# S's products between the pieces of the logits, in a graph attention and nucleus diffusion kernel

## The chip, the cores and the metric

The kernel runs on one core of one Trainium2 chip. The metric is the device time of an execution in microseconds; runs of one kernel are compared by their median.

## The reference

The input is 2708 rows of 512 features and a dense 2708 x 2708 adjacency of zeros and ones. Two layers follow each other. The first is graph attention with eight heads. The second, which the change touches, makes two steps of diffusion. In a step it builds an attention matrix that keeps, in each row, only the largest weights whose sum reaches 0.9 of the row (the nucleus), and it moves three copies of the features: forward and backward with the adjacency, and with the attention matrix.

```python
S = S + jnp.eye(n, dtype=X.dtype)
Rf = S / jnp.clip(S.sum(axis=1, keepdims=True), 1e-12)
Rb = S / jnp.clip(S.sum(axis=0), 1e-12)[:, None]
Xf, Xb, Xa = (X, X, X)
for s in range(STEPS):                     # STEPS = 2
    A = _adj_from_feats(Xa, W1, W2, W3)    # logits, nucleus of 0.9, softmax
    Xf = Rf @ Xf
    Xb = Rb @ Xb
    Xa = A @ Xa
    Z = Z + (Xf @ U1[s] + Xb @ U2[s] + Xa @ U3[s])
Y = X + Z                                  # and a layer norm
```

## The kernel before

Rows are cut into 22 tiles of 128 (the last has 20 rows). A pair is two tiles, a quad four; there are 11 pairs and 6 quads, the last quad of two tiles. Each of the two steps (s = 0 and 1, the flag `last` is the second) runs a loop over g from -1 to 10 in which three pairs are in work at once.

- **Logits of pair g + 2** (`Logits.products`, L513): for each of the two tiles six pieces of 452 columns, each two matmuls into a PSUM tile of `ps_t` (two buffers, tile name `t`) and a copy by ScalarE into the tile `p` (four buffers, so the pair's tiles are those of pair g, whose search must be over).
- **Search for pair g + 1** (`search`, L598): VectorE looks for the threshold of each row. It takes the row's maximum of pair g + 2 on the way (`nmx`, L548), and ends in `finish` with a branch (L890). Its results are the tiles `keep`. In its middle it calls `early` and, before `finish`, `late`, which put other engines' work and some of VectorE's into the program there.
- **Attention of pair g** (`attended`, L1005): twelve groups, six for each tile of the pair. A group transposes up to four blocks of `keep` for the next group (L1016), has ScalarE copy them (tile `at`, L1020), and multiplies those of its own with `va` (L1035). From the fourth group on it also issues steps of `fills`, ScalarE's passes over the logits of pair g + 2 (`exp`, L526): for each tile a root and a full exponential, and then twelve looks (L553), which wait for the thresholds `nth` from GpSimd.
- **Mix of pair g** (`mixed`, L1060): three times four steps over the weights U (L1076), each step followed by one step of `others`, and three fills in each of the first two times.
- **S products** (`part`, L943): the steps of the list `others`. One S product loads 128 rows of the features (`hl`, 512 KB, three buffers) and of S (`s_r`, 256 KB) and makes eight matmuls into four PSUM tiles (L967). In the first step one S product serves both directions, a quad has 22 of them over two iterations, and after the second half, at odd g, eight steps `scaled` follow: ScalarE scales a PSUM tile into `xe` (L977), GpSimd's queue writes it out, VectorE splits it into a high and a low part (L181, L182), and GpSimd's queue writes these. In the second step an iteration has 22 S products and four `scaled`, without the splits.
- **Order of the queues**: inside the step the programs of TensorE, ScalarE, VectorE and the DMA queue of SyncE are in the order in which the code issues them (`manual_schedule`). `paced(steps, n)` issues the next n steps of a list. `diffused` loads the four rows tiles `x` that the mix needs.

In the kernel before, all pieces of a block come one after another, then the queries of pair g + 3 are loaded, and the steps of `others` are issued in the attention groups and in the mix. In the first step a group of the pair's first tile issues one and a group of its second tile two; in the second step only the second tile's groups issue some, two each:

```python
if not last:
    paced(others, 1 + i)
elif i or len(grp) == 1:
    paced(others, (total + 10) // 13)
```

Of the kernel before, what the change touches and what calls it, by code (L numbers as in the profile page):

```python
# [53 lines left out]
def kernel(  # L54
# [37 lines left out]
    pairs = [list(range(g, min(g + G, NT))) for g in range(0, NT, G)]  # L92
# [399 lines left out]
    class Logits:  # L492
# [17 lines left out]
                                      in_=kq_d[self.s][DA:, :, t * P:(t + 1) * P])  # L510
                self.q.append(q)

        def products(self):  # L513
            wide, small, ps_l = self.pools
            for q, t in zip(self.q, self.grp):
                pr = rows[t]
                p = wide.tile([P, N], F32, name="p", bufs=4)
                for c0, c1 in chunks:
                    pl = ps_l.tile([P, 512], F32, name="t")
                    for i in range(2):  # L520
                        nc.tensor.matmul(pl[:, :c1 - c0], lhsT=q[:, i], rhs=self.keys[:, c0:c1],  # L521
                                         start=(i == 0), stop=(i == 1))
                    nc.scalar.copy(p[:pr, c0:c1], pl[:pr, :c1 - c0])  # L523
                self.p.append(p)

        def exp(self, looks=True):  # L526
# [387 lines left out]
    for s in range(STEPS):  # L914
        last = s == STEPS - 1
        with ExitStack() as st:
# [18 lines left out]
            def values():  # L935
                for t in range(NT):
                    nc.sync.dma_start(out=va[:rows[t], t, :], in_=(xa_d if last else va_d)[cols[t], :])
# [53 lines left out]
            def paced(steps, n):  # L991
                for step in steps[:n]:
                    step()
                del steps[:n]

            def diffused(grp):
                out_ = []
                for i in range(2):
                    for t in grp:
                        x = work.tile([P, D], F32, name=f"x{i}")  # L1000
                        nc.sync.dma_start(out=x[:rows[t]], in_=xfb_d[i, cols[t], :])
                        out_.append(x)
                return out_[:len(grp)], out_[len(grp):]

            def attended(grp, keep, rden, fills, others, then):  # L1005

                def turned(i, t, cs):
                    pr = rows[t]
                    pt = ps_t.tile([P, TG, P], F32, name="t")
                    at = work.tile([P, TG, P], F32, name="at")
                    for j, c in enumerate(cs):
                        nc.tensor.transpose(pt[:rows[c], j, :pr], keep[i][:pr, cols[c]], ident[:pr, :pr])  # L1016
                    full = sum(rows[c] == P for c in cs)
                    for r, j0, j1 in ((P, 0, full), (rows[cs[-1]], full, len(cs))):
                        if j0 < j1:
                            nc.scalar.copy(at[:r, j0:j1, :pr], pt[:r, j0:j1, :pr])  # L1020
                    return at

                steps = [(i, t, cs) for i, t in enumerate(grp) for cs in tgroups]
                at = turned(*steps[0])
                xa = []
                total = len(others)
                for n, (i, t, cs) in enumerate(steps):
                    pr = rows[t]
                    nxt = turned(*steps[n + 1]) if n + 1 < len(steps) else then()
                    if n >= 3:  # L1030
                        paced(fills, 1 + i if last else 1 if n > 8 else 2)
                    if cs[0] == 0:
                        pa = ps_a.tile([P, D], F32, name="a")
                    for j, c in enumerate(cs):
                        nc.tensor.matmul(pa[:pr], lhsT=at[:rows[c], j, :pr], rhs=va[:rows[c], c, :],  # L1035
                                         start=(c == 0), stop=(c == NT - 1))
                    if not last:
                        paced(others, 1 + i)
                    elif i or len(grp) == 1:
                        paced(others, (total + 10) // 13)  # L1040
                    if cs[-1] == NT - 1:
                        xa.append(work.tile([P, D], F32, name="xa"))
                        nc.scalar.activation(xa[i][:pr], pa[:pr], AF.Copy, scale=rden[:pr, i:i + 1])  # L1043
                        if not last:
                            nc.gpsimd.dma_start(out=xa_d[cols[t], :], in_=xa[i][:pr])
                    at = nxt
                    yield
                return xa, at
# [8 lines left out]
            def turned_rows(grp, v):  # L1057
                return [transposed(up, ps_t, v[i], rows[t], "v_t") for i, t in enumerate(grp)]
# [105 lines left out]
            with tc.manual_schedule(engines={PE, ACT, DVE, SP}):  # L1164
                counted, spread = ranks() if last else (None, None)
                lg = [Logits(pools, s, grp, keys, rank) for grp in pairs[:1]]
                lg[0].queries()
                lg[0].products()
                steps = lg[0].exp(looks=False)
                if last:  # L1170
                    counted()
                for step in steps:
                    step()
                half = []
                lg += [Logits(pools, s, grp, keys, rank) for grp in pairs[1:2]]
                lg[1].queries()
                for step in part(half, 0):
                    step()
                values()
                done = []  # L1180
                ready = None
                looks, left = [], []
                for g in range(-1, NP):

                    fills = []

                    held = len(left)
                    paced(left, held if last else held // 2)
                    others = left + part(half, g + 2)
                    left = []  # L1190
                    if g == 0 and last:
                        paced(others, 4)
                    if g + 2 < NP:
                        lg[g + 2].products()
                    if g + 3 < NP:
                        lg.append(Logits(pools, s, pairs[g + 3], keys, rank))
                        lg[g + 3].queries()
                    norms = [normed(t, y) for t, y in done] if last else []
                    done = []

                    rows_in = []
                    if g >= 0:
                        others.insert(0 if g else len(others) // 3, lambda g=g: rows_in.extend(diffused(pairs[g])))
                        final = g == NP - 1 and not last
                        att = attended(pairs[g], *ready, fills, others,
                                       lambda: None if final else turned_rows(pairs[g], rows_in[0]))
                    if g == 0:

                        paced(others, held - held // 2 if not last else 0)
                        while looks:  # L1210
                            next(att)
                            paced(looks, 2)

                    def early(g=g):
                        if g + 2 < NP:
                            fills.extend(lg[g + 2].exp())
                        return lambda: [rest() for rest in norms]

                    def late(g=g):
                        if g >= 0:  # L1220
                            if g:
                                paced(others, 1)
                            xa, v_t = rest_of(att)
                            done.extend(mixed(pairs[g], v_t, *rows_in, xa, others, fills, final))
                            paced(others, len(others))
                            paced(fills, len(fills))
                            return


                        if last:  # L1230
                            spread()
                        paced(fills, 5 + G * NA)
                        paced(others, NT if last else NT - NT // 2)
                        looks.extend(fills)
                        left.extend(others)

                    if g + 1 < NP:
                        ready = search(lg[g + 1], g >= 0, early, late)
                    else:
                        for rest in norms:  # L1240
                            rest()
                        late()
                if last:
                    for rest in [normed(t, y) for t, y in done]:
                        rest()
# [31 lines left out]
```

## Time and profile before

| what | value |
|---|---|
| median of 3 runs | 3711.15 us (3710.86 to 3714.24) |
| the profiled execution | 3711.47 us, span 3709.7 us |
| busy share of the span | PE 91%, DVE 70%, ACT 42%, POOL 22% |
| mean granted clock of TensorE | 0.963 |
| first step, g = 1 to 8: start of a block of logits to the next | 101.9 to 109.4 us |
| second step, g = 1 to 8, the same | 115.5 to 117.5 us |

The span runs from the first to the last instruction. PE is TensorE, ACT is ScalarE, DVE is VectorE, POOL is GpSimd and SP is SyncE; an engine's name with a q is its sequencer. In a row of groups the first number after the bar is the busy time, the second the mean of one instruction in ns, and after the second bar stands the idle time of the engine just before these instructions, with what ended it. In a timeline the columns are start, duration, engine, line, operation, operands, and in brackets the idle time before and what ended it. The ends of matmuls are modelled, so distances between starts are used here where a pace is meant. The windows give for each stretch the busy time of PE, its weight loads, DVE, ACT and POOL, the granted clock, the share of the DMA engines and GB/s.

The first step of the second layer runs from 1095 to 2304 us of the span, the second from 2304 us to its end.

### The profile page before, as it was taken

Reading aid. Unit: us, or ns where it says so; the run is one execution under the profiler, and the core shown is the slowest. Engines: PE = TensorE matmul, PEld = TensorE weight load, DVE = VectorE, ACT = ScalarE, POOL = GpSimd, SP = SyncE. Lnnn points to the kernel's source line nnn. Section 1 sums busy time; section 2 is a strip of 40 time slices with the busy share of each in tenths; the row PEclk is TensorE's granted clock in tenths of the full one; section 3 lists DMA queues with packets and bytes.
Section 4 is the critical chain, followed back from the end, with each engine's and each line's share of the span. In section 5 each row is a group of like instructions: output and inputs, shape, how many; then the busy total and the mean of one; then the engine's idle time right before and its main releaser. Section 6 shows DMA issues by size and latency. Waiting matters only on the chain. (4 is left out here: it accounts for less than half of the span.)

```text
span 3709.7 us, 35331 instructions
## 1 busy us (share of the span) xinstructions
PE 3376.1 (91%) x11143; PEld 1757.7 (47%) x11143; DVE 2612.0 (70%) x4820; ACT 1541.7 (42%) x2334; POOL 808.4 (22%) x1119
## 2 busy tenths in 40 slices
PE   7998999998956898989899899678999999999898
PEld 4432333333434455545455453445555565556452
DVE  4587888989947537374454652958978779777991
ACT  2343212111124764555666612335654556445511
POOL 4114240514331121121211121301112112121101
PEclk9999999999978999999999999999999999999999
DMA  3476424233237454454545353855655666566652
GB/s 113 152 251 239 141 79 151 82 104 106 70 99 274 139 195 166 156 179 148 199 149 189 122 193 104 302 191 195 206 188 205 234 216 204 184 212 234 202 200 66
DMA packets 276458, 634.08 MB, mean 171 GB/s; under 512 B 37209, under 2 KB 70441, under 8 KB 273243
## 3 DMA queue, kind: packets, MB, share of 16 engines
q1 hardware_dynamic: 249183, 540.99, 44.4%
q0 software_dynamic: 27024, 90.30, 6.4%
q8 instruction: 89, 1.46, 0.2%
q14 instruction: 162, 1.33, 0.1%
HBM read 509.07 MB, written 122.10 MB: 170 GB/s over the span
## 5 line engine op out<-in xcount | busy, mean ns | idle before, releaser
L1035 PE MATMUL a<-va,at 128*128 128x512 f32 (+2 forms) x1936 | 895.6, 602 | 39.6 <-ACT at L1020 39.5
L967 PE MATMUL q<-hl,s_r 128*128 128x512 f32 x2904 | 824.5, 430 | 61.1 <-DMA s_r<-s_d 60.9
L429 PE MATMUL po<-e,fw 128*65 128x512 f32 (+4 forms) x2112 | 838.9, 552 | 32.9 <-DVE e L427 23.3
L427 DVE SCALAR_TENSOR_TENSOR e<-r_b,kk,a_c 128x512 f32<-128x512 f32 (+4 forms) x1056 | 751.1, 740 | 68.5 <-PE po L429 18.1
L967 PEld LDWEIGHTS q<-hl,s_r 128*128 128x128 f32 x2904 | 547.9, 191 | 306.3 <-issue 135.4
L553 ACT ACTIVATE junk_a<-p,nth 128x2708 uint8<-128x2708 f32 (+1 forms) x240 | 613.2, 2555 | 68.8 <-POOL nth L572 65.1
L429 PEld LDWEIGHTS po<-e,fw 128*65 128x65 f32 (+1 forms) x2112 | 285.9, 139 | 546.6 <-issue 270.8
L1035 PEld LDWEIGHTS a<-va,at 128*128 128x128 f32 (+2 forms) x1936 | 339.2, 188 | 408.5 <-issue 346.7
L1076 PE MATMUL a<-u_k,v_t 128*128 128x512 f32 (+1 forms) x1056 | 491.4, 603 | 19.6 <-ACT xa L1043 14.4
L629 DVE SCALAR_TENSOR_TENSOR junk<-p,th 128x2708 bf16<-128x2708 f32 (+1 forms) x132 | 401.3, 3040 | 4.0
L1020 ACT COPY at<-t 128x512 f32<-128x512 f32 (+3 forms) x308 | 140.4, 477 | 478.6 <-PE t L1016 478.4
L1076 PEld LDWEIGHTS a<-u_k,v_t 128*128 128x128 f32 (+1 forms) x1056 | 189.4, 187 | 240.6 <-issue 183.8
L521 PE MATMUL t<-keys,q_t 128*128 128x452 f32 x528 | 165.3, 439 | 94.7 <-ACT p L523 73.6
L181 DVE TENSOR_SCALAR split_hl<-xe 128x512 int32<-128x512 int32 (+1 forms) x44 | 19.1, 434 | 263.4 <-ACT xe L977 217.0
L808 DVE MAX8 vn<-keep 128x8 f32<-128x2708 f32 (+1 forms) x66 | 196.8, 2981 | 2.3
L523 ACT COPY p<-t 128x452 f32<-128x452 f32 (+2 forms) x264 | 132.2, 539 | 123.2 <-PE t L521 85.6
L411 ACT ACTIVATE s_c<-a_c 128x512 fp32r<-128x512 f32 (+3 forms) x132 | 76.2, 578 | 250.1 <-DMA a_c<-in_adj_t_dram 124.8
L1016 PE MATMUL t<-ident,keep 128*128 128x128 f32 (+1 forms) x968 | 147.4, 274 | 26.4 <-DVE keep L757 18.8
L521 PEld LDWEIGHTS t<-keys,q_t 128*128 128x128 f32 x528 | 90.1, 208 | 165.4 <-ACT p L523 126.4
L1016 PEld LDWEIGHTS t<-ident,keep 128*128 128x128 f32 (+1 forms) x968 | 115.0, 139 | 106.8 <-issue 78.6
L548 DVE TENSOR_REDUCE nmx<-p 128x1 f32<-128x2708 f32 (+1 forms) x44 | 129.1, 2966 | 43.4 <-ACT p L523 43.4
L565 POOL TENSOR_TENSOR x<-sums,powers 128x4 f32<-128x4 f32 x22 | 43.7, 1987 | 507.9 <-ACT p L560 481.9
(296 smaller groups left out, 3160.6 us busy)
## 6 DMA issues: line engine op xcount, KB each, us to landing
s_r<-s_d SPq DMA_DIRECT2D x330, 256.0 KB
hl<-vhl_d SPq DMA_DIRECT2D x132, 512.0 KB
u_k<-in_L_gnn_U_dram SPq DMA_DIRECT2D x264, 256.0 KB
hl<-fhl_d SPq DMA_DIRECT2D x132, 512.0 KB
hl<-bhl_d SPq DMA_DIRECT2D x132, 512.0 KB
arow<-in_adj_dram SPq DMA_DIRECT2D x21, 1354.0 KB
s_d<-s_c SPq DMA_DIRECT2D x88, 256.0 KB
a_c<-in_adj_t_dram SPq DMA_DIRECT2D x84, 256.0 KB
```

The source lines that it names most:

```text
L427: nc.vector.scalar_tensor_tensor(e[:pr, :cw], r_b[:pr, i, :cw], kk[:pr, t, hd:hd + 1], a_c[t][:pr, :cw], op0=OP.max, op1=OP.mult)
L429: nc.tensor.matmul(po[i][:, :cw], lhsT=fw[:pr, t, hd, :], rhs=e[:pr, :cw], start=(t == 0), stop=(t == NT - 1))
L521: nc.tensor.matmul(pl[:, :c1 - c0], lhsT=q[:, i], rhs=self.keys[:, c0:c1], start=(i == 0), stop=(i == 1))
L523: nc.scalar.copy(p[:pr, c0:c1], pl[:pr, :c1 - c0])
L553: nc.scalar.activation(junk[:pr], self.p[i][:pr], func, **kw)
L629: v.scalar_tensor_tensor(junk_b[:pr], ps_[i][:pr], th, ps_[i][:pr], op0=OP.is_ge, op1=OP.mult, accum_out=dst)
L808: v.max(vs, keep[0][:pr])
L967: nc.tensor.matmul(half[j], lhsT=s_r[:, j * P:(j + 1) * P], rhs=hl[:, h], start=(c == 0 and h == 0), stop=(c == NT - 1 and h == 1))
L1016: nc.tensor.transpose(pt[:rows[c], j, :pr], keep[i][:pr, cols[c]], ident[:pr, :pr])
L1020: nc.scalar.copy(at[:r, j0:j1, :pr], pt[:r, j0:j1, :pr])
L1035: nc.tensor.matmul(pa[:pr], lhsT=at[:rows[c], j, :pr], rhs=va[:rows[c], c, :], start=(c == 0), stop=(c == NT - 1))
L1076: nc.tensor.matmul(pz[i][:rows[t]], lhsT=v_t[i][:, k, :rows[t]], rhs=u_k, start=(n == 0 and k == 0), stop=(n == 2 and k == KD - 1))
```

## The change

From g = 1 on, the loads of `diffused` and one S product are issued ahead of the block of logits, and after every second piece one more S product is issued, six in a block. For the first tile of a pair an attention group of the first step now issues no step of `others`, for the second tile one instead of two. `diffused` is put at the head of `others` before the block instead of after it, and `late` issues it only where it has not been issued before (g = 9 and 10).

```diff
@@ class Logits @@
-        def products(self):
+        def products(self, between=lambda: None):
+
             wide, small, ps_l = self.pools
+            pieces = 0
             for q, t in zip(self.q, self.grp):
...
                     nc.scalar.copy(p[:pr, c0:c1], pl[:pr, :c1 - c0])
+                    pieces += 1
+                    if pieces % 2 == 0:
+                        between()
                 self.p.append(p)
@@ attended @@
                     if not last:
-                        paced(others, 1 + i)
+                        paced(others, i)
                     elif i or len(grp) == 1:
                         paced(others, (total + 10) // 13)
@@ the loop over g @@
                     if g == 0 and last:
                         paced(others, 4)
+
+                    rows_in = []
+                    if g >= 0:
+                        others.insert(0 if g else len(others) // 3, lambda g=g: rows_in.extend(diffused(pairs[g])))
                     if g + 2 < NP:
-                        lg[g + 2].products()
+                        if g > 0:
+                            paced(others, 2)
+                        lg[g + 2].products((lambda: paced(others, 1)) if g > 0 else lambda: None)
                     if g + 3 < NP:
                         lg.append(Logits(pools, s, pairs[g + 3], keys, rank))
                         lg[g + 3].queries()
                     norms = [normed(t, y) for t, y in done] if last else []
                     done = []
-
-                    rows_in = []
                     if g >= 0:
-                        others.insert(0 if g else len(others) // 3, lambda g=g: rows_in.extend(diffused(pairs[g])))
                         final = g == NP - 1 and not last
@@ late @@
                         if g >= 0:
-                            if g:
+                            if g and not rows_in:
                                 paced(others, 1)
```

## The prediction

> **What bounds the kernel now.** The page first: PE is busy 91% of the span, so I read what PE does between the blocks of logits, and who holds it up. In section 5 of the page the pieces of the logits and their evictions (busy, mean ns | idle before, releaser):
>
> ```profile
> L521 PE MATMUL t<-keys,q_t 128*128 128x452 f32 x528 | 165.3, 439 | 94.7 <-ACT p L523 73.6 <-DMA q_t<-kq_d 19.1
> L523 ACT COPY p<-t 128x452 f32<-128x452 f32 (+2 forms) x264 | 132.2, 539 | 123.2 <-PE t L521 85.6 <-DVEq L890 36.4 <-DVE ends L653 0.3
> ```
>
> PE waits for the evictions, and these, 36.4 us of the time, for the search on DVE (L890 is its last branch). The timeline of PE shows both kinds of block. In the second step (g = 4, an ordinary block):
>
> ```profile
> 2942.90 1.39 PE L521 MATMUL t<-keys,q_t 128*128 128x452 f32 x4
> 2945.73 1.12 PE L521 MATMUL t<-keys,q_t 128*128 128x452 f32 x4 [1.45 <-ACT p L523]
> 2947.05 1.11 PE L521 MATMUL t<-keys,q_t 128*128 128x452 f32 x4 [0.19 <-ACT p L523]
> ...
> 2952.27 1.10 PE L1016 MATMUL t<-ident,keep 128*128 128x128 f32 x8 [0.18 <-ACT p L523]
> ```
>
> 9.4 us for 24 matmuls that PE can start every 0.207 us (in the trace at 2943.51, 2943.72, 2943.92): with two PSUM tiles, ACT's copies of 0.54 us set the pace. In the first step, g = 4:
>
> ```profile
> 1622.12 1.46 PE L521 MATMUL t<-keys,q_t 128*128 128x452 f32 x4
> 1631.68 7.51 PE L521 MATMUL t<-keys,q_t 128*128 128x452 f32 x20 [8.11 <-ACT p L523]
> 1639.09 1.38 PE L1016 MATMUL t<-ident,keep 128*128 128x128 f32 x8
> ```
>
> and the timelines of DVE and ACT say why:
>
> ```profile
> 1602.98 0.69 DVE L182 TENSOR_TENSOR split_hl<-xe,split_hl 128x512 f32<-128x512 f32 x1
> 1603.59 3.03 DVE L806 SCALAR_TENSOR_TENSOR keep<-p,th 128x2708 f32<-128x2708 f32 x1
> ...
> 1629.59 0.14 DVE L887 TENSOR_SCALAR code_i<-code 1x1 int32<-1x1 f32 x1
> ```
> ```profile
> 1631.09 0.97 ACT L523 COPY p<-t 128x452 f32<-128x452 f32 x2 [7.28 <-DVEq L890]
> ```
>
> In an odd g of the first step DVE splits eight scaled rows, and only then ends the search; PE's third piece starts 28.0 us after the last split's end (1603.67 to 1631.68). So **every second block of the first step hangs on the chain S products, xe copies, splits, search**, not on PE.
>
> **What the Trainium skill says.** "Perfetto Trace Analysis", section "Tensor Engine Instruction (MATMUL, LD_WEIGHTS)": ACT, DVE and GPSIMD queues are strict FIFO. The trace agrees: DVE stands 42.81 us in front of the first split at 1583.46 with the search behind it. "DMA: Bandwidth & Descriptors", section "Anatomy of one DMA": a DMA's semaphore wait is on the issuing sequencer. The trace agrees: SP's timeline has no issue from 2935.3 to 2944.62, where the xb load waits for its tile, then twelve in 7 us. "Perfetto Trace Analysis", section "Roofline": about 435 GB/s for 16 DMA engines; the windows 1524 to 1528 read 409.
>
> **Prices.** One S product is 8 matmuls 0.23 us apart, 1.84 us (an attention step with two takes 7.56 us, 2861.69 to 2869.25, one without 3.88, 2840.45 to 2844.33; half of 3.68). Back to back S products come every 2.56 us (11 in 28.16 us from 1149.38), their loads being the limit at three buffers. Two pieces cost PE 4 x 0.207 = 0.83 us. A root, full or look pass on ACT is 2.68 us with its accumulator read. I call T0 the first transpose (L1016) of an iteration, X its start.
>
> **What changes, counted.** For g = 1 to 8: one S product before the pieces, six between them. First step: of 11 S products 7 then come before T0 and 4 in the second row tile's groups; the first tile's groups get none, and in odd g the scaled rows move to the last two groups (2) and the mix (6). At g = 0 and 9 no S product is ahead of T0; six move from the attention groups to the mix. Second step: (19 + 10)//13 is still 2, so the groups keep 12 and only the mix gives up 7. On SP the x loads and S loads pass the query loads and, in the second step, the xb loads; those are wanted only an iteration, or some 20 us, later: nothing. POOL gets the same DMAs, later: counted with the splits.
>
> **1. Second step, g = 1 to 8.** Now: 9.38 + 7 x 1.84 = 22.3 us. After: 1.84 + 6 x (0.83 + 1.84) = 17.9 if nothing waits. But the first S load stands behind the last u_k, two y_d and four x loads and is issued, at SP's pace of now, some 3.5 us before X. In the block at 1518.84 the x loads and three S products, 3.4 MB, go from 1514.65 to 1529, the first S product by its place among the bytes landing near 1524, 6 us after its issue at 1517.94 (an estimate). So PE waits 2.5 to 3 us: 20.9, gain 1.4 x 8 = **-11 us**. Bounds: no wait, 4.4 x 8 = -35; each of the seven loads late by another 0.3, +6. On DVE, nmx starts 7.1 us after the last copy now (2952.66 to 2959.76), which the longer block just uses up, and DVE idles 9.8 us at the iteration's end: no loss there.
>
> **2. First step, ACT in the attention groups.** Without S products a group is 3.9 us of PE, but ACT has two passes and a copy, 6.1 us. At g = 8, where products have run out, it shows:
>
> ```profile
> 2105.74 3.70 PE L1035 MATMUL a<-va,at 128*128 128x512 f32 x8 [0.44 <-ACT at L1020]
> 2109.27 0.38 PE L1016 MATMUL t<-ident,keep 128*128 128x128 f32 x2
> 2111.43 3.70 PE L1035 MATMUL a<-va,at 128*128 128x512 f32 x8 [1.77 <-ACT at L1020]
> ```
>
> Stepped from T0: PE reaches group 3 at 12.6 and group 6 at 23.0. ACT has group 4's copy at 13.9, then four passes with a copy among them, to 25.6, then group 6's copy, 26.1: PE waits 3.1. The looks need nth from POOL, 6.4 us after the last pass (1880.97 to 1887.55 now, less the read): six of them from 32.0 to 49, and PE waits 0.4 to 0.7 for the copies in groups 8, 9 and 10. Attention ends at 57 (64 now, with seven more S products), the mix and project at 80.5 (even g) or 83.1 (odd g; 94.5 now). This is inside steps 3 to 5.
>
> **3. Odd g to even g.** Looks, scaled copies (xe, 0.68) and v_t copies (0.57) are one queue on ACT. From group 9's copy at 49.7: look 52.4, copy, look 55.5, xe 56.2, two v_t, look 60.1, xe 60.7, xa, two v_t 62.6; then xe and look three times, 72.6, xe 73.3, two v_t 74.5, xe, xe 75.9. The last split ends at 79.6 (a split waits 3.9 us for the write of the second before it), against 76.1 now. PE's third piece is then at T0 + 107.6; PE itself is there at 83.1 + 5.3, after two S products and two pieces. Then come ten pieces with five S products, 5 x 2.67 = 13.3, and the clock. After such a wait PE stays at half speed for a while, as now:
>
> ```profile
> 1842.00:1850.00 8.00, 6.99 (x20) 4.15 (x20) 3.52 (x28) 5.39 (x11) 0.00 (x0) 0.70 0.09 36
> ```
>
> (0.70 is the granted clock: 4.8 of the 8 us at half, 2.4 lost; now hidden by ACT's copies.) T0 to next T0: 107.6 + 15.7 = 123.3, against 112.6, 111.5 and 113.2 (mean 112.4): +10.9. Even to odd: 80.5 + 17.9 + 2.5 of load wait = 100.9, against 98.2: +2.7. Three pairs: **+41**. At g = 8 the S products are half as long: 118.8 against 111.7, then some 80 against 83.2: **+4**. Bounds: the last split 5 us earlier or later, 20 us either way.
>
> **4. g = 0 to 1.** PE now stands 10.3 us before 1248.36 for ACT, with five S products ahead of that wait; they come behind it instead: 9.2, less the 1.9 that ACT waits for PE at 1212.93, and 1 for groups like those of 2: +8.3. The first block of g = 1 grows from 8.73 to 20.4: +11.7. **+20**.
>
> **5. g = 9 to 10.** Now the splits end at 2198.15, 54.8 after T0, and PE, at 2223.47, finds the search just done. After, the last S product is in the mix at T0 + 66, the fourth split ends at 76, the search 25.3 later at 101.3; PE is there at 80.1 and has no S product left. 20.5 more, and 2.4 of clock: **+23** (15 to 27).
>
> **Sum:** -11 + 41 + 4 + 20 + 23 = +77 on the profiled execution's 3711.47 (span 3709.7 and 1.8 around it), which is 0.3 above the median: 3788.
>
> **Rivals.** *The loads come in time* (for: 409 GB/s at the peak; against: x and y_d go first): 24 us in step 1 and 10 in the odd blocks go, 3754; chance 0.22 with its neighbours down to 3720. *The search is not the gate*, and it ends faster: steps 3 and 5 hang on the last scaled copy at T0 + 75.9. Each us that ACT brings it earlier saves some 5 us (three pairs, g = 7 to 8, g = 9 to 10). From 15 us earlier, six looks of 2.68 us fewer ahead of it, the sign turns; at 22 us earlier it is 3788 - 110 = 3678. For: the blocks' own idle, 94.7 us, is then gain. Against: ACT's one queue has the looks first. 0.12. *Worse:* the second step's DVE chain, whose slack is the 9.8 us above, is pushed by late p copies, 5 us in each of 8 iterations: 3828; 0.10. *It does nothing:* waits only change their name, 3711; 0.05. The forecast itself, 3770 to 3810: 0.51.
>
> **Numbers.** About 0.2%, 7 us, can be told from no change. The range, 3712 to 3825, leaves out the faster case, some half of the same and half of the worse one (0.2), and takes in the bounds of steps 1, 3 and 5 but for the corners where all fall on one side. Faster 0.12, same 0.05, slower 0.83.
>
> **What would show it.** Right: x20 of L521 after odd g of the first step becomes runs of 4 with L967 between, after a wait of some 20 us for p L523 with L890 behind it (L523 <- DVEq L890 from 36.4 to above 90); PE waits some 20 us for the search once, at g = 10; L1035 <- at L1020 rises from 39.5 by some 40; the blocks of the second step take 20 to 21 us from first S product to T0 and their iterations 114 to 116 instead of 116.7. Wrong: the splits of an odd g ending before T0 + 65, or even blocks that wait no longer than 8 to 11 us.

## The result, and the profile after

The changed kernel takes 3826.8 us (median of 4 runs, 3825.56 to 3837.11) against 3712.69 us for the kernel before on the same chip: a ratio of 1.0315, 95% interval 1.0301 to 1.033, so 114 us slower. The forecast of 3788 us had the sign right and the first step of the layer nearly so; it was 39 us short, and the time lies just above the range's end of 3825. The error is almost all in the second step, where step 1 of the prediction failed. The profiled execution has a span of 3825.2 us against 3709.7, and these two are compared below.

Lines after the change are those of before plus 2 (the pieces), 5 (search, attention, mix, S products) or more. The groups by line of the changed kernel (after the bars: busy, mean ns, then the idle time before and who ended it):

```profile
L1040 PE MATMUL a<-va,at 128*128 128x512 f32 (+2 forms) x1936 | 909.1, 609 | 66.6 <-ACT at L1025 66.6
L972 PE MATMUL q<-hl,s_r 128*128 128x512 f32 x2904 | 815.4, 427 | 118.1 <-DMA s_r<-s_d 117.6
...
L523 PE MATMUL t<-keys,q_t 128*128 128x452 f32 x528 | 148.2, 407 | 92.0 <-ACT p L525 71.7 <-DMA q_t<-kq_d 20.3
...
L525 ACT COPY p<-t 128x452 f32<-128x452 f32 (+2 forms) x264 | 130.1, 538 | 347.8 <-PE t L523 258.3 <-DVEq L895 82.0 <-DVE cur L671 7.2
```

Two of these groups in the kernel before (the pieces and their copies stand in the prediction):

```profile
L1035 PE MATMUL a<-va,at 128*128 128x512 f32 (+2 forms) x1936 | 895.6, 602 | 39.6 <-ACT at L1020 39.5
L967 PE MATMUL q<-hl,s_r 128*128 128x512 f32 x2904 | 824.5, 430 | 61.1 <-DMA s_r<-s_d 60.9
```

Three readings. PE's wait for the pieces' copies is as long as before (92.0 for 94.7), although S products now lie between the pieces: the copies now wait 82.0 us for the search on DVE (L895), where it was 36.4 (L890 then). PE's wait for the loads of the S products has doubled (118.1; it was 61.1). And the attention groups wait 27 us longer for their own copies (66.6; it was 39.6).

The iterations, from T0 (the first transpose of an iteration) to the next T0, say where the time went (us):

| iterations | before | forecast | after |
|---|---|---|---|
| first step, g = 1, 3, 5 | 112.6, 111.5, 113.2 | 123.3 | 124.0, 124.2, 122.3 |
| first step, g = 2, 4, 6 | 98.5, 98.1, 98.1 | 100.9 | 100.2, 101.2, 101.6 |
| first step, g = 7, 8 | 111.7, 83.2 | 118.8, 80 | 120.3, 80.5 |
| first step, g = 0 | 117.5 | +20 | 139.4 |
| first step, g = 9 | 80.1 | +23 | 104.3 |
| second step, mean of g = 1 to 6 | 117.0 | 115.6 | 119.2 |

The first step lost 93 us where 88 was forecast. The second step lost 21 us, all differences of its iterations added, where a gain of 11 was forecast. This is the whole error but for some 7 us. The six iterations of the last row give 13 of the 21: that of g = 0 has the first longer block and no shorter mix (146.6 for 128.6), that of g = 8 a shorter mix and no block (101.0 for 112.4).

**The search, in the first step.** The timeline of PE in the changed kernel, from the end of the mix of g = 3 to the next T0:

```profile
1652.57 2.57 PE L972 MATMUL q<-hl,s_r 128*128 128x512 f32 x8 [2.44 <-DMA s_r<-s_d]
1654.93 1.71 PE L523 MATMUL t<-keys,q_t 128*128 128x452 f32 x4
1656.44 2.45 PE L972 MATMUL q<-hl,s_r 128*128 128x512 f32 x8
1671.91 1.88 PE L523 MATMUL t<-keys,q_t 128*128 128x452 f32 x4 [13.02 <-ACT p L525]
1673.59 3.62 PE L972 MATMUL q<-hl,s_r 128*128 128x512 f32 x8
1677.00 1.38 PE L523 MATMUL t<-keys,q_t 128*128 128x452 f32 x4
...
1688.05 1.04 PE L1021 MATMUL t<-ident,keep 128*128 128x128 f32 x8
```

The third piece waits 13.02 us, and the other ten pieces, with the five S products between them, come behind the wait. That the wait is for the search, and the search for the splits, the timelines of ACT and DVE show:

```profile
1634.20 0.78 ACT L982 ACTIVATE xe<-q,rinv 128x512 f32<-128x512 f32 x1
1634.78 0.78 ACT L982 ACTIVATE xe<-q,cinv 128x512 f32<-128x512 f32 x1
...
1671.32 0.97 ACT L525 COPY p<-t 128x452 f32<-128x452 f32 x2 [19.75 <-DVEq L895]
```
```profile
1641.70 0.43 DVE L181 TENSOR_SCALAR split_hl<-xe 128x512 int32<-128x512 int32 x1 [3.23 <-DMA bhl_d<-split_hl]
1642.17 0.69 DVE L182 TENSOR_TENSOR split_hl<-xe,split_hl 128x512 f32<-128x512 f32 x1
1642.78 3.03 DVE L811 SCALAR_TENSOR_TENSOR keep<-p,th 128x2708 f32<-128x2708 f32 x1
```

With T0 at 1563.9 the last scaled copy ends at +71.7, the last split at +79.0, and the third piece starts at +108.0, 29.1 us after that split.

**The S loads, in the second step.** PE and SP at the start of an ordinary block (for the T0 of g = 4):

```profile
3034.67 12.61 PE L1081 MATMUL a<-u_k,v_t 128*128 128x512 f32 x29
3052.57 3.75 PE L972 MATMUL q<-hl,s_r 128*128 128x512 f32 x8 [5.29 <-DMA s_r<-s_d]
3056.12 1.31 PE L523 MATMUL t<-keys,q_t 128*128 128x452 f32 x4
3057.27 2.02 PE L972 MATMUL q<-hl,s_r 128*128 128x512 f32 x8
3059.12 0.98 PE L523 MATMUL t<-keys,q_t 128*128 128x452 f32 x4
3059.94 2.01 PE L972 MATMUL q<-hl,s_r 128*128 128x512 f32 x8
```
```profile
3032.70 8.07 SPq L1079 DMA_DIRECT2D u_k<-in_L_gnn_U_dram  x5
3040.82 1.76 SPq L1097 DMA_DIRECT2D xw<-y_d  x2
3042.62 1.86 SPq L1006 DMA_DIRECT2D x<-xfb_d  x4
3044.54 0.46 SPq L966 DMA_DIRECT2D hl<-fhl_d  x1
```

The first S product waits 5.29 us for its load, starts 8.0 us after that load was issued, and then runs at half speed: from its start to the first piece 3.55 us, where the next one takes 1.85. In the six blocks of g = 2 to 7 this wait is 3.3 to 5.3 us, 4.1 in the mean; the block shown has the longest of these (that of g = 1 waits 7.0). From there on a unit is 2.67 us (3057.27 to 3059.94), as forecast. In the windows of the same place the columns after the five engines are the granted clock, the share of the DMA engines and GB/s:

```profile
3042.00:3044.00 2.00, 2.00 (x6) 0.91 (x5) 0.00 (x0) 0.00 (x0) 0.00 (x0) 1.00 0.91 268
3044.00:3046.00 2.00, 2.00 (x6) 0.93 (x5) 0.00 (x0) 0.00 (x0) 0.00 (x0) 1.00 0.89 274
3046.00:3048.00 2.00, 1.27 (x3) 0.21 (x2) 0.00 (x0) 1.17 (x2) 0.88 (x1) 1.00 0.91 298
...
3050.00:3052.00 2.00, 0.00 (x0) 0.00 (x0) 1.72 (x15) 0.00 (x0) 1.35 (x3) 0.50 1.03 408
```

The DMA engines are busy from the y_d and x loads on, but move under 300 GB/s until 3048; and at 3050 the clock is already at 0.50.

### The profile page after: what moved, and what is told of

Same layout as the page of the kernel before. It is cut to its first block, busy times and chain, and to the rows that moved or that the text cites. A ratio compares the mean times of both kernels' runs of the same rounds, so it can differ in the third digit from the quotient of the medians.

```text
span 3825.2 us, 35329 instructions
## 1 busy us (share of the span) xinstructions
PE 3386.5 (89%) x11143; PEld 1789.6 (47%) x11143; DVE 2616.7 (68%) x4820; ACT 1538.9 (40%) x2334; POOL 784.0 (20%) x1119
## 5 line engine op out<-in xcount | busy, mean ns | idle before, releaser
L1040 PE MATMUL a<-va,at 128*128 128x512 f32 (+2 forms) x1936 | 909.1, 609 | 66.6 <-ACT at L1025 66.6
L972 PE MATMUL q<-hl,s_r 128*128 128x512 f32 x2904 | 815.4, 427 | 118.1 <-DMA s_r<-s_d 117.6
L972 PEld LDWEIGHTS q<-hl,s_r 128*128 128x128 f32 x2904 | 559.2, 195 | 334.5 <-issue 112.2
L1040 PEld LDWEIGHTS a<-va,at 128*128 128x128 f32 (+2 forms) x1936 | 343.7, 190 | 446.2 <-issue 359.7
L1081 PE MATMUL a<-u_k,v_t 128*128 128x512 f32 (+1 forms) x1056 | 485.7, 600 | 25.5 <-DMA u_k<-in_L_gnn_U_dram 17.2
L1025 ACT COPY at<-t 128x512 f32<-128x512 f32 (+3 forms) x308 | 139.9, 475 | 437.7 <-PE t L1021 437.7
L523 PE MATMUL t<-keys,q_t 128*128 128x452 f32 x528 | 148.2, 407 | 92.0 <-ACT p L525 71.7
L1021 PE MATMUL t<-ident,keep 128*128 128x128 f32 (+1 forms) x968 | 147.2, 275 | 41.1 <-DVEq L895 29.1
L523 PEld LDWEIGHTS t<-keys,q_t 128*128 128x128 f32 x528 | 105.0, 209 | 125.0 <-ACT p L525 87.1
```

The lines of the kernel that those rows point to most:

```text
L972: nc.tensor.matmul(half[j], lhsT=s_r[:, j * P:(j + 1) * P], rhs=hl[:, h], start=(c == 0 and h == 0), stop=(c == NT - 1 and h == 1))
L1081: nc.tensor.matmul(pz[i][:rows[t]], lhsT=v_t[i][:, k, :rows[t]], rhs=u_k, start=(n == 0 and k == 0), stop=(n == 2 and k == KD - 1))
```

## The experiments

Seven kernels were timed beside the kernel before: the first four below have ratios to a median of 3711.59 us, the last three to 3712.86 us.

**Attention groups alone.** The kernel before with fewer S products in the groups, nothing else:

```diff
-                        paced(others, 1 + i)
+                        paced(others, i)
```

> The kernel before with the second part of the change alone: in the first step the attention groups of a pair's first tile issue no step of others and those of the second tile one; nothing is put between the pieces. Theory (ScalarE's one queue and the splits behind it set the first step): at odd g the eleventh S product is now in the mix at T0 + 79, the eight scaled copies and splits follow at some 2.4 us each, so the last split ends near T0 + 99 and the next T0 comes at 134 instead of 112; even g waits for ScalarE's looks and loses 3 to 4; g = 9 to 10 loses 23, g = 0 to 1 loses 8. Sum some +130: 3840 us, second step unchanged. Rival (the S products ahead of the attention are what costs, by delaying it): without them the time stays within 3705 to 3740.

Measured: 3877.83 us, ratio 1.0448 (1.0426 to 1.047), some 166 us slower, nearly all of it in the first step (iterations of odd g 139.9 to 142.9 us, second step unchanged). The row of the copies, and the timelines of PE and of ACT of this kernel, at the iteration before the T0 of 1712.90:

```profile
L523 ACT COPY p<-t 128x452 f32<-128x452 f32 (+2 forms) x264 | 132.0, 539 | 227.3 <-DVEq L890 141.9 <-PE t L521 82.7 <-DVE ends L653 0.7
```
```profile
1669.45 1.45 PE L521 MATMUL t<-keys,q_t 128*128 128x452 f32 x4
1705.45 7.51 PE L521 MATMUL t<-keys,q_t 128*128 128x452 f32 x20 [34.54 <-ACT p L523]
1712.90 1.34 PE L1016 MATMUL t<-ident,keep 128*128 128x128 f32 x8
```
```profile
1661.33 0.69 ACT L977 ACTIVATE xe<-q,rinv 128x512 f32<-128x512 f32 x1 [4.56 <-DMA xfb_d<-xe]
1668.84 0.27 ACT L165 COPY kq_hl<-t 128x128 f32<-128x128 f32 x1 [6.83 <-PE t L160]
...
1671.01 0.72 ACT L977 ACTIVATE xe<-q,cinv 128x512 f32<-128x512 f32 x1
```

The theory's direction holds and its size was 38 us too low. The last split ends 106.2 to 109.1 us after T0: the last of the eleven S products of an odd g is now at +78 to +81, and the last of the eight scaled copies ends some 19 us after it. The looks are over by then; the copies wait for their own buffers to be written out (4.56 us for the seventh), and the eighth stands on ACT's queue behind the copies of the projection, which wait 6.83 us for PE's mix to end. The splits trail by 8 to 10 us. Then 25.9 us of search, and a block with nothing else to do for PE. Thinning the groups alone is worse than the whole change: the block's S products repay a part of it.

**Blocks alone.** The changed kernel with the old pace in the groups:

```diff
-                        paced(others, i)
+                        paced(others, 1 + i)
```

> The changed kernel with the old pacing of the attention groups, 1 + i: seven S products in each block of logits, and the rest as early in the groups as they were before. Theory: at odd g the four S products left are in groups 0 to 3, the scaled steps in groups 4 to 8, the last split ends near T0 + 60, the search near T0 + 88, before TensorE is at the pieces (T0 + 92): no wait for the search in even blocks, T0 to T0 near 112 at odd g, and g = 9 to 10 costs nothing again. Even g still waits for ScalarE's looks, 104 instead of 98. First step +30 instead of +95, second step as in the changed kernel (+21): some 3763 us, 3745 to 3775. Rival (the interleave itself costs the time, by late loads and the slow clock after waits): above 3800.

Measured: 3765.57 us, ratio 1.0148 (1.013 to 1.0167), within the 3745 to 3775 us of the theory. The timeline of PE in the same block as above, and the row of the copies:

```profile
1644.28 3.66 PE L972 MATMUL q<-hl,s_r 128*128 128x512 f32 x8 [2.37 <-DMA s_r<-s_d]
1647.78 0.99 PE L523 MATMUL t<-keys,q_t 128*128 128x452 f32 x4
1648.61 1.99 PE L972 MATMUL q<-hl,s_r 128*128 128x512 f32 x8
1650.43 0.98 PE L523 MATMUL t<-keys,q_t 128*128 128x452 f32 x4
```
```profile
L525 ACT COPY p<-t 128x452 f32<-128x452 f32 (+2 forms) x264 | 129.8, 538 | 281.9 <-PE t L523 269.8 <-DVE fr L669 6.8 <-DVEq L895 5.1
```

No wait for the search is left in the block: the copies stand 5.1 us for L895. The last S product of an odd g before its block is at T0 + 23.6 and the last split at + 58.1 to 58.3; at g = 9 the iteration is 79.9 us, what it was. So the wait of 13 us and the 24 us of g = 9 come from the thinner groups, not from the blocks. But this kernel is 54 us slower than the one before, too: some 17 us in the second step (the sum of its iterations), 14 us at g = 0, and 9 to 10 us in the even g from 2 to 6 of the first step, whose groups now wait for ACT (L1040 stands 97.1 us for L1025).

**The x loads behind.** The changed kernel; in the second step the four x loads are issued behind the block's seven S products:

```diff
-  others.insert(0 if g else len(others) // 3, ...
+  others.insert((7 if last else 0) if g else len(others) // 3, ...
-                            paced(others, 2)
+                            paced(others, 1 if last else 2)
```

> The changed kernel, with the four x loads of an iteration of the second step issued behind the block's seven S products instead of ahead of them; first step as in the change. Theory (the first S load is late because u_k, y_d and x, 1.8 MB, go ahead of it, and the wait brings half a clock): the first load is issued 1.9 us earlier with 1 MB less ahead of it, the wait of 5.3 us at the block's first S product falls under 2 and the slow clock goes: 4 to 6 us in each of 8 iterations, 3780 to 3795. Rival (the S loads themselves cannot keep the block's pace): the wait moves to the third or fourth S product of the block, gain under 10 us, 3817 or more.

Measured: 3798.54 us, ratio 1.0232 (1.0214 to 1.025), 28 us below the changed kernel and a little above the 3780 to 3795 us of the theory. The second-step blocks, from the last mix matmul to T0, fall from 24.9 to 20.6 us (means of six), and the iterations by the same 4.3 us, from 119.2 to 114.9. The profiled execution (span 3815.1 us) was some 18 us longer than the median, and its first step longer than the changed kernel's by as much; only its second step is read here.

**Three loads early, in one burst.** The changed kernel; the first three S loads of the next iteration are issued in the last third of the second step's mix, each directly ahead of the load of a u_k (`part` split into loads and products):

```diff
+                        if n == 2 and k < 3:
+                            paced(ahead, 1)
                         u_k = up.tile([P, D], F32, name="u_k", bufs=4 if last else 3)
                         nc.sync.dma_start(out=u_k, in_=u[s, k * P:(k + 1) * P, :])
...
```

> The changed kernel, with the loads of the first three S products of the next iteration issued in the mix of the second step, ahead of the last time's first three u_k loads; products where they were. Theory (as for the x loads): they land before the block, which takes 18 us from first S product to T0 instead of 25: 6 us in each of 8 iterations, near 3775. Rival: u_k comes late instead and TensorE waits in the mix (L1081 for u_k, 17 us now, rises by 20 or more), total within 15 us of 3827.

Measured: 3818.66 us, ratio 1.0281 (1.0262 to 1.0301): the rival. The blocks fell to 18.2 to 18.6 us as the theory said, the mix rose from 26.6 to between 30.0 and 33.4, and PE's wait for u_k from 17.2 us to 43.8. The end of a mix in the timeline of PE (L1097 is the mix in this kernel, L986 the S products):

```profile
3047.64 1.98 PE L1097 MATMUL a<-u_k,v_t 128*128 128x512 f32 x4 [0.66 <-DMA u_k<-in_L_gnn_U_dram]
3053.37 5.20 PE L1097 MATMUL a<-u_k,v_t 128*128 128x512 f32 x8 [3.74 <-DMA u_k<-in_L_gnn_U_dram]
3058.00 2.40 PE L986 MATMUL q<-hl,s_r 128*128 128x512 f32 x8
```

The weights u_k now stand behind the S loads: the wait has moved one stage up, and the clock has gone to half there (0.50 from 3053.00 to 3056.41; 5.20 us for eight matmuls).

**The second step alone.** The first step as before, with the old pace in its groups and its x loads where they were; S products between the pieces only where `last`:

```diff
...
+                        if last and g > 0:
+                            paced(others, 2)
+                        lg[g + 2].products((lambda: paced(others, 1)) if last and g > 0 else lambda: None)
```

> The first step is as before; only the second step's S products of a block stand between the pieces, as in the change. Theory (the first S load of a block comes late behind the last u_k, two y_d and four x loads, whatever the first step does): the blocks of the second step still take 24 to 26 us, the second step costs some 21 us as in the changed kernel and the first step nothing, so 3730 to 3737 us. Rival (the second step's loss was a consequence of the first step's new order, and step 1 of the prediction holds by itself): blocks of 21 us and 3701 us.

Measured: 3732.27 us, ratio 1.0055 (1.0041 to 1.0068). As the theory said: 19 us slower by itself, iterations 118.2 us (mean of g = 1 to 6), blocks of 22.2 to 25.5 us, first step as in the kernel before. The failure of step 1 of the prediction doesn't come from the first step of the layer.

**The second step alone, x loads behind.** The edits of the two kernels together.

> As the one before, with the four x loads of a second-step iteration issued behind the block's seven S products instead of ahead of them, and one step instead of two ahead of the pieces. Theory: the gain of 28 us that this had on the changed kernel is had here too, blocks of 20 to 22 us, 3702 to 3710 us: within 0.3% of the kernel before. Rival (what was gained there came from the first step, or the x rows now come too late for the transposes of v_t): no better than second_only.

Measured: 3699.72 us, ratio 0.9964 (0.9953 to 0.9974): 13 us faster than the kernel before, a little under what was expected. SP and PE at the block for the T0 of g = 4:

```profile
2936.71 1.52 SPq L1097 DMA_DIRECT2D xw<-y_d  x2
2938.27 0.47 SPq L966 DMA_DIRECT2D hl<-fhl_d  x1
```
```profile
2945.21 2.09 PE L972 MATMUL q<-hl,s_r 128*128 128x512 f32 x8 [1.95 <-DMA s_r<-s_d]
2947.14 0.98 PE L523 MATMUL t<-keys,q_t 128*128 128x452 f32 x4
2947.96 2.02 PE L972 MATMUL q<-hl,s_r 128*128 128x512 f32 x8
```

The load still goes behind y_d and u_k, but PE waits for it 1.95 us here and 1.2 in the mean of the six blocks, against 3.7 in the kernel before this one. The S product after it runs at full speed: the granted clock is 1.00 from 2606 to 3476 us. From the first S product to T0 five of the six blocks take 17.8 to 17.9 us. The x rows come in time: from T0 to the mix it stays at 67.7 us.

**The second step alone, three loads spread over the mix.** As the kernel of three early loads, with the first step of before, and one load every three weight steps, each behind the load of a u_k:

```diff
+                        if (n, k) in ((1, 0), (1, 3), (2, 2)):
+                            paced(ahead, 1)
```

> As second_only, with the first three S loads of a block issued during the mix of the iteration before, one every three weight steps, instead of after it. Theory (the block needs its first three loads early, and the mix has DMA room for 2.4 MB in 26 us if they don't come in one burst): blocks of 18 us with a mix that stays at 26.5 to 28 us, T0 to T0 112 to 113 us instead of 118 to 119, 3675 to 3695 us, faster than the kernel before. Rival (any load in the mix holds up the weights u_k behind it on the same queue, as in the burst): mix of 30 us or more, 3705 to 3725 us.

Measured: 3698.19 us, ratio 0.9962 (0.9948 to 0.9975). Faster than the kernel before the change and than the changed one, and not to be told from the second step alone with the x loads behind. It is 3 us above what was expected. PE at the seam (L1097 is the mix, L986 the S products):

```profile
2921.47 12.18 PE L1097 MATMUL a<-u_k,v_t 128*128 128x512 f32 x28
2935.71 1.99 PE L1097 MATMUL a<-u_k,v_t 128*128 128x512 f32 x4 [2.05 <-DMA u_k<-in_L_gnn_U_dram]
2937.13 2.42 PE L986 MATMUL q<-hl,s_r 128*128 128x512 f32 x8
2939.39 0.98 PE L523 MATMUL t<-keys,q_t 128*128 128x452 f32 x4
```

The block starts without a wait and takes 18.2 us in five of six iterations, but one u_k still comes 2.05 us late, the mix is 27.7 to 28.9 us, and T0 to T0 is 114.6 us, not 112 to 113.

## Why the prediction was right in the first step and wrong in the second

**Step 1 failed, in the term of the load wait and by a term that it left out.** Its sum was 3 us of wait for the first S load and 17.9 us from there to T0, 20.9 in all. Measured, as means of g = 2 to 7: 4.7 us from the start of the mix's last matmul to the first S product, and 20.2 us from there to T0, 24.9 in all. So each block misses 1.7 us of wait and 2.3 us behind it; the eight blocks together are 30 us longer than forecast.

*The wait.* The prediction had the load issued 3.5 us before PE comes, and there 6 us after the issue. In the block shown it was issued 2.7 us before PE had ended its mix (3044.54 to 3047.28), and the S product started 8.0 us after the issue. The 6 us came from a block of the first step, where only the four x loads go directly ahead; here two y_d loads and the last u_k do as well, and the windows read 268 to 298 GB/s. The Trainium skill, "DMA: Bandwidth & Descriptors", section "Queues, rings and completion order", says that on each DMA engine descriptors are consumed in ring order. The trace agrees: the packets of hl, the only ones of 4 KB that move on SP's queue here, begin at 3048.25, 3.7 us after the issue, and until then packets of 2 KB go, the size of the rows ahead. That the x loads are part of it is shown: in the second step alone, with them behind, the mean wait falls from 3.7 to 1.2 us.

*The clock.* Steps 3 and 5 counted 2.4 us of half speed after a wait of PE; step 1 counted none. It is the larger part: with the clock at 1.00, the second step alone with the x loads behind takes the 17.9 us that the step had said. The Trainium skill, "TensorE: Matmul & The Clock Gate", section "Part 1: The HAM clock gate", says that the clock drops to half after an idle window of some 3.4 us, and that this window runs freely. The trace agrees on the second point: in the changed kernel half speed begins at 2691.62, 2814.50, 2930.55 and 3050.02, whole multiples of 3.413 us apart (36, 34 and 35). On the first the measurement differs, and it decides: with the x loads behind, a wait of 1.93 us brought half speed (eight matmuls in 3.03 us from 3057.04), while in the second step alone one of 3.29 us did not (2.06 us from 2718.11). Half speed can also come late: after the wait of 2.44 us shown above it begins at 1653.97, and it is the piece (1.71 us) and the next S product (2.45) that it slows. What decides was not worked out.

The bound of +6 us, seven loads each late by 0.3, had looked in the wrong place: the later loads are not late, the first alone is. And the sign given for a right forecast, 20 to 21 us from the first S product to T0, came out (20.2) by luck: the step's own sum has 17.9 there, and the rest is the clock.

**Step 2** was right in kind and too high: the rise of the groups' wait for their copies is 27 us, not 40. **Step 3** came within a microsecond, by errors that cancel: the last scaled copy was at T0 + 71.7, not 75.9, and the splits trailed it by some 7 us, not 3.7, since a split waits up to 3.2 us for the write of an earlier one and these waits add up. PE itself reached the third piece at T0 + 95.0, not 88.4, so that its wait is 13 us instead of some 20; that cost nothing, as the search ends later still. The sum over three pairs is +41.5 for +41. **Steps 4 and 5** measured +21.8 for +20 and +24.3 for +23; the wait of step 5 (20.5 in its sum, though its own figures, 101.3 less 80.1, give 21.2), with no S product left for PE, stands alone in the trace:

```profile
2318.29 1.94 PE L1021 MATMUL t<-ident,keep 128*128 128x128 f32 x8 [22.02 <-DVEq L895]
```

g = 7 and 8 came to +5.9 for +4.

**The rivals.** *Loads come in time* was the wrong way round for the change as it stands, and right as a statement of what is to be had: with the load waits gone or short the interleaved second step beats the old one, by 13 to 15 us. *The search is not the gate* fell with the 13.02 us wait; the kernel with the blocks alone shows that the mechanism exists, with the splits 21 us earlier and no wait, but the thinner groups forbid it. And with the old groups the first step is still slower than it was before the change: the waits for S loads in the block, the half clock after some of them and the waits for ACT in the groups take more than the gain. *Worse* named about the right time, 3828, for the wrong reason: DVE. In the kernel with the x loads behind, the iterations fall by what the blocks fall, 4.3 us, so the second step still hangs on PE and its loads. *It does nothing* fell.

**What stays open.** Why y_d, x and u_k move at under 300 GB/s with the DMA engines busy nine tenths of the time, where hl and s_r reach 408, was not tried. Nor was a kernel tried with spread loads and late x loads together, or one with the blocks of the first step freed of their load waits.

## What to carry to other kernels

Work moved to the front of a stage brings its loads with it: read on the DMA queue what is issued ahead of the first of them, and take its landing from a place with the same loads ahead; one late first load cost 4.1 us of wait in the mean, and 2.3 us of slow clock on top. Filling a wait with other work gains nothing while the same queue order makes the work that ends the wait later: here the groups that were thinned to supply the filler ended the splits 79 us after T0 instead of 58, and the wait came back. When a load is pulled forward, spread it: three loads in one burst gave most of their gain back in the stage above, the same three one by one kept most of it. The spread ones also start earlier and stand behind a u_k instead of ahead of it; which of these did it was not separated. And two halves of a change need not add: the blocks alone cost 54 us and the groups alone 166, both together 114.

## What the runs showed of the hardware that was not expected

- Half speed of TensorE does not go by the length of the wait: 1.93 us brought it, 3.29 us did not, and 2.44 us brought it only 1.4 us after the wait had ended. It begins only at whole multiples of 3.413 us from one another.
- A busy DMA is not a fast one: at a busy share of 0.89 to 0.91 the windows show 268 to 298 GB/s, and 408 at 1.03.
